# Pacing the row gathers of a two-layer graph attention kernel: a wait for the gather two ahead in place of a memset between gathers

## The chip, the core and the metric

The kernel runs on one core of one Trainium2 chip. The metric is the device time in microseconds (us) of one launch. Engines are named as in the profile: PE is TensorE (PEld its weight loads), DVE is VectorE, ACT is ScalarE, POOL is GpSimd, SP is SyncE. Each engine has an instruction queue of its own; "POOLq" in a row means an instruction that the queue itself handled, such as a wait on a semaphore.

## The reference, cut to what matters

Two graph attention layers run on N = 6250 nodes with D = 256 features and E = 200000 edges, which come sorted by their destination node. Layer 0 has four heads, layer 1 has one. For each edge the layer needs the transformed row of the source node:

```python
hx = (x @ Wg).reshape(n, h, f)
al = leaky_relu(s_src[src] + s_dst[dst] + s_edge, 0.2)      # one logit per edge and head
m = segment_max(al, dst)
al = exp(al - m[dst])
al = al / segment_sum(al, dst)[dst]
out = segment_sum(hx[src] * al[:, :, None], dst)             # the rows of all sources, weighted
x = out + b + x                                              # layer 0 has a relu around it
```

The edge term comes from a small network on 32 edge features. Each node also has a loop edge to itself, whose edge feature is the mean over its incoming edges.

## The kernel before, in words

A prologue writes, for every node, one table row into device memory: `T0` for layer 0 (268 floats: the 256 features of `hx` and a few scalars), later `T1` for layer 1 (260 floats are read of each row). The edges are then worked through in steps of `P * C` = 128 x 24 edges. There are 66 steps in each layer; the last two are shorter (14 and 13 chunks). An edge of a step lies on one of 128 partitions, in one of 24 chunks.

`gather(st)` fetches the table rows of a step's source nodes into a tile `G` of 128 x 24 x 270 floats. It issues one indirect DMA per chunk from the POOL queue (L799): 128 rows, one for each partition, named by a column of the index tile `src`. The last chunk of a step goes first, then chunks 0 to 22. After each such gather, POOL runs a memset of a scratch tile `gap`, 128 x 208 floats (L803), that nothing reads. The very first step is not gathered from the table: the prologue fetches its rows of `x` with 24 indirect DMAs of its own (L249), without memsets between them. So L799 runs 3102 times in all.

There are three buffers for `G` (`gp[k % 3]`). The whole schedule is written out by hand; each engine takes its instructions in program order. In the loop of `edges`, the gather of step k+1 is issued first. Then come the logits of step k on DVE (L987 is the first instruction that reads `G`), the scans and the running maxima per destination, the scaling of the gathered rows in place (L1095, DVE, it writes columns 0 to 255 of `G`), and the sums as 24 matmuls with one-hot matrices (L1105, PE). ACT copies the sums out of PSUM (L1110), and the finishing work of the step before follows on DVE and ACT. The loads of the coming steps (`ea`, `lb`, `tw`) and the stores of finished rows (`T<-t1row` in layer 0 at L1239, `out` in layer 1) go through SP's queue.

Semaphores are placed by the framework. The gathers go round eight completion semaphores in turn, and a gather's completion counts 16 increments on its semaphore. A gather waits for the gather eight before it, which used the same semaphore; the first one of a step also waits for the last readers of its buffer. Where an instruction has several waits, the last one stands in the instruction itself, and the others are put before it on its queue as `EVENT_SEMAPHORE` instructions; these are seen in the trace as POOLq rows.

Between the layers (`ending`) POOL does the finishing of two steps (14 elementwise instructions, L1178 to L1192), and the first gather of layer 1 waits until `T1` is written. At the end two indirect DMAs on POOL store the last two steps' rows (L1249).

Of the kernel before, what the change touches and what calls it, by code (L numbers as in the profile page):

```python
# [22 lines left out]
F32 = mybir.dt.float32  # L23
# [8 lines left out]
P = 128  # L32
C = 24
SE = P * C
NX = 24
D = 256
ED = 32
PH = 64
# [18 lines left out]
class Layer:  # L57
# [3 lines left out]
    def __init__(self, l):  # L61
        self.l = l
        self.H = H = HEADS[l]
        self.F = D // H
        self.p = D
        self.g = D + H
        self.one = D + H + 1
        self.gr = self.ad = D + H + 2
        self.m = self.ln = D + 2 * H + 2
        self.W = D + 3 * H + 2  # L70
# [9 lines left out]
class Kernel:  # L80
# [122 lines left out]
    def prologue(self):  # L203
# [4 lines left out]
        GT = 7  # L208
        CX = self.CX = min(self.cs[0], NX)
        V = nc.vector  # L210
# [192 lines left out]
    def fixed_rows(self):  # L403
        nc, cp = self.nc, self.cp
        self.crow = cp.tile([1, D + self.L[0].H], F32, name="crow")
        self.cl = [cp.tile([36, P + 1], F32, name=f"cl{i}") for i in range(2)]
        for t in self.cl:
            nc.gpsimd.memset(t, -BIG)

        self.cnt = cp.tile([P, self.NS, 2], F32, name="cnt")  # L410
        self.mt = cp.tile([P, 4 * C + 4], F32, name="mt")
        self.gap = cp.tile([P, 208], F32, name="gap")
        self.fb = [cp.tile([P, 37 * C], F32, name=f"fb{i}") for i in range(2)]
        for t in [self.mt] + self.fb:
            nc.gpsimd.memset(t, 0.0)


        self.aq = [cp.tile([P, 4, 32], BF, name=f"aq{i}") for i in range(2)]
        for t in self.aq:
            nc.gpsimd.memset(t, 0.0)  # L420
        self.trow1 = []
        L1 = self.L[1]
        for i in range(2):
            self.trow1.append(cp.tile([P, 2 * L1.TW], F32, name=f"t1row{i}"))
            nc.gpsimd.memset(self.trow1[i][:, L1.TW + D:], 0.0)
# [366 lines left out]
    def gather(self, st):  # L792
        nc, L = self.nc, st["L"]
        st["G"] = G = self.G0 if st["k"] == 0 else self.gp[st["k"] % 3].tile([P, C, 270], F32, name="G")
        n = self.N
        idx = self.src[:, st["o"]:st["o"] + st["C"]]
        last = st["C"] - 1
        for c in (range(0) if st["k"] == 0 and self.CX > last else (last, *range(last))):
            nc.gpsimd.indirect_dma_start(  # L799
                out=G[:, c, 0:L.TW], out_offset=None, in_=self.rows[L.l][0:n * (1 + L.l), :],  # L800
                in_offset=bass.IndirectOffsetOnAxis(ap=idx[:, c:c + 1], axis=0))
            if st["k"]:
                nc.gpsimd.memset(self.gap, 0.0)  # L803

    def pair(self, k):

# [660 lines left out]
```

## Time and profile before

| | before |
|---|---|
| median of 3 runs | 4556.34 us (4555.35 to 4557.77) |
| the profiled execution: time | 4555.93 us |
| its span | 4554.1 us |
| mean granted TensorE clock | 0.743 |
| POOL busy | 3915.8 us (86%) |
| PE busy | 3065.9 us (67%) |
| DVE busy | 2901.8 us (64%) |
| ACT busy | 516.8 us (11%) |
| gathers of L799 | 3102, from 89.3 to 4511.8 us |
| memsets of L803 | 3102 |
| busy share of the DMA engines by the gathers' queue | 35.2% |
| the same by the queue of SP | 10.0% |

The profile is of one execution. Its time is 1.8 us above its span, and 0.4 us below the median of the runs. Busy time counts an engine's own work; a POOL row for an indirect DMA covers the making of its descriptors, not the moving of the data, which the DMA engines do afterwards. The trace holds the landing of each DMA on its semaphore beside this.

### The profile page before, as it was taken

To read this page: it belongs to the slowest core of one execution; us is meant where nothing else is said; L and a number is where in the kernel's file an instruction comes from. 1 tells how busy PE (TensorE), PEld (TensorE's weight loads), DVE (VectorE), ACT (ScalarE), POOL (GpSimd) and SP (SyncE) were. 2 spreads that over 40 slices of the span, in tenths; PEclk is the share of its full clock that TensorE was granted. 3 is DMA by queue.
4 is the path that set the end of the run, shared out by engine and by line. 5 is a ranking of instruction groups with operands and counts; after the bars stand their busy time and mean duration, and the time that the engine had idled before them with its cause. 6 is when DMAs were issued, how large, how long until landed. Compare 5 with 4: busy or idle time off the path is not lost. (4 is left out here: it accounts for less than half of the span.)

```text
span 4554.1 us, 37613 instructions
## 1 busy us (share of the span) xinstructions
PE 3065.9 (67%) x9916; PEld 1899.5 (42%) x9916; DVE 2901.8 (64%) x6675; ACT 516.8 (11%) x1150; POOL 3915.8 (86%) x6365
## 2 busy tenths in 40 slices
PE   8777677667677677677746566666666665666665
PEld 6444444444444344444424334333343343433433
DVE  7877667677677677676745555555554555555655
ACT  5111111111111111111100000000000000000000
POOL 6888888888888888888878888888888888888885
PEclk9877777777777777777767777777777777777777
DMA  6444444444444444444434444444444444444442
GB/s 224 130 136 134 126 129 136 124 127 136 125 128 135 125 128 135 125 130 134 119 98 124 116 128 122 118 128 128 111 128 121 124 123 128 122 116 122 128 116 74
DMA packets 231112, 576.39 MB, mean 127 GB/s; under 512 B 63097, under 2 KB 87871, under 8 KB 230825
## 3 DMA queue, kind: packets, MB, share of 16 engines
q0 software_dynamic: 150144, 422.75, 35.2%
q1 hardware_dynamic: 80331, 150.52, 10.0%
q8 instruction: 79, 1.29, 0.1%
q14 instruction: 142, 1.16, 0.1%
q10 hardware_dynamic: 416, 0.67, 0.1%
HBM read 542.72 MB, written 31.09 MB: 126 GB/s over the span
## 5 line engine op out<-in xcount | busy, mean ns | idle before, releaser
L799 POOL DMA_INDIRECT G<-T,src x3102 | 2969.6, 957 | 553.1 <-issue 518.7
L1105 PE MATMUL u<-G,S 128*128 128x270 f32 (+1 forms) x6252 | 1461.0, 393 | 106.7 <-DVE G L1085 97.6
L1105 PEld LDWEIGHTS u<-G,S 128*128 128x128 f32 x6252 | 1189.5, 192 | 388.0 <-DVE G L1085 162.1
L803 POOL MEMSET gap<- 128x208 f32 x3102 | 893.3, 288 | 1.8
L1095 DVE TENSOR_TENSOR G<-G,kps 128x6144 f32<-128x6144 f32 (+3 forms) x136 | 853.0, 6274 | 0.0
L885 PE MATMUL y<-ea,webd 64*128 64x384 f32 (+1 forms) x1056 | 749.7, 860 | 67.3 <-ACT R L890 66.7
L1010 PE MATMUL lf<-ident,fb 128*36 128x128 f32 (+1 forms) x132 | 53.3, 404 | 1093.3 <-DVE fb L1002 772.3
L987 DVE TENSOR_TENSOR G<-rt,G 128x96 f32<-128x96 f32 (+1 forms) x132 | 30.2, 228 | 1138.9 <-DMA G<-T,src 1138.6
L1010 PEld LDWEIGHTS lf<-ident,fb 128*36 128x36 f32 (+1 forms) x132 | 15.7, 119 | 1134.6 <-DVE fb L1002 819.2
L899 PE MATMUL zad<-R,wea 128*64 128x384 f32 (+1 forms) x1056 | 476.0, 815 | 0.5 <-DVE aq L952 0.3
L890 ACT ACTIVATE R<-y,webd 128x768 f32<-128x768 f32 x260 | 233.2, 897 | 2015.2 <-PE lf L1027 1647.7
L930 DVE TENSOR_TENSOR S<-kps,loc 128x3072 f32<-128x3072 f32 x132 | 437.5, 3315 | 4.5
L885 PEld LDWEIGHTS y<-ea,webd 64*128 64x128 f32 x1056 | 300.9, 314 | 311.8 <-issue 192.5
L899 PEld LDWEIGHTS zad<-R,wea 128*64 128x64 f32 x1056 | 160.7, 207 | 319.0 <-issue 214.0
L945 PE MATMUL zad<-a,Q 128*128 128x12 bf16 (+1 forms) x132 | 24.9, 188 | 174.6 <-DVE a L943 174.6
L430 PE MATMUL fin<-wg,h1T 128*128 128x260 f32 x264 | 135.3, 667 | 2.3 <-ACT h1T L1200 2.3
L973 DVE STREAM_TRANSPOSE rt<-zad 128x768 f32<-128x768 f32 (+1 forms) x130 | 124.9, 960 | 12.1 <-PE zad L959 11.2
L914 DVE TENSOR_TENSOR lb<-lb,kps 128x1536 bf16<-128x1536 bf16 (+1 forms) x68 | 112.7, 1658 | 0.0
L1110 ACT ACTIVATE U<-u 128x270 f32<-128x270 f32 (+1 forms) x132 | 51.9, 393 | 493.7 <-PE u L1105 493.7
L1041 DVE SCALAR_TENSOR_TENSOR m<-fpen,lf,m 128x24 f32<-128x24 bf16 (+1 forms) x66 | 16.4, 249 | 132.8 <-PE lf L1027 132.6
L945 PEld LDWEIGHTS <-Q 128*128 128x128 bf16 x132 | 13.7, 104 | 208.3 <-DVE a L943 198.6
L430 PEld LDWEIGHTS fin<-wg,h1T 128*128 128x128 f32 x264 | 75.6, 316 | 52.1 <-issue 36.6
(201 smaller groups left out, 2287.5 us busy)
## 6 DMA issues: line engine op xcount, KB each, us to landing
G<-T,src POOLq DMA_INDIRECT x3102, 2.8
ea<-in_ea_dram SPq DMA_DIRECT2D x64, 768.0 KB
lb<-locrow SPq DMA_DIRECT2D x64, 384.0 KB
T<-t1row SPq DMA_DIRECT2D x66, 227.5 KB
tw<-T SPq DMA_DIRECT2D x66, 225.8 KB
tw<-T SPq DMA_DIRECT2D x66, 117.2 KB
tw<-in_x_dram SPq DMA_DIRECT2D x66, 112.0 KB
out_dram<-fb SPq DMA_DIRECT2D x64, 112.0 KB
```

What stands on the lines that cost most here:

```text
L430: self.nc.tensor.matmul(ps[:, :L.MW], hT[:, k, :], self.wg[L.l][:, k, :], start=(k == 0), stop=(k == 1))
L799: nc.gpsimd.indirect_dma_start(out=G[:, c, 0:L.TW], out_offset=None, in_=self.rows[L.l][0:n * (1 + L.l), :], in_offset=bass.IndirectOffset ...
L803: nc.gpsimd.memset(self.gap, 0.0)
L885: nc.tensor.matmul(y[:, o], self.webd[l][r, :], ea[r, w], start=True, stop=True)
L890: nc.scalar.activation(R[:, i, :32 * c].rearrange("p (b n) -> p b n", b=2), y.rearrange("p (b n) -> p b n", b=2)[:, :, :16 * c], AF.Relu, ...
L899: nc.tensor.matmul(st["zad"][i * PH:(i + 1) * PH, o], self.wea[l][0], R[:, i, w], start=True, stop=False)
L914: V.tensor_tensor(lb[:, :, :n], lb[:, :, :n], self.k_part.unsqueeze(2).to_broadcast([P, i, n]), op=OP.is_equal)
L930: nc.vector.tensor_tensor(st["S"][:, c0:c1, :], self.k_iota.unsqueeze(1).to_broadcast(w), self.loc[:, o + c0:o + c1].unsqueeze(2).to_broad ...
L973: V.transpose(rv[:, :32 * c].rearrange("p (b n) -> p b n", b=2), z.rearrange("p (b n) -> p b n", b=2)[:, :, :16 * c])
L1010: self.nc.tensor.transpose(self.lf[0:e.shape[1], 1:P + 1], e, self.ident)
L1095: nc.vector.tensor_tensor(v, v, pw[:, c0:c1, :].unsqueeze(3) .to_broadcast([P, c1 - c0, H, L.F]), op=OP.mult)
L1105: nc.tensor.matmul(st["u"][:, :L.W], S[:, i, :], G[:, i, 0:L.W], start=(j == 0), stop=(j == c - 1))
```

## The change

Each gather of L799 from the third on is preceded by a copy on POOL of one element per partition (128 x 1) of the gather issued two before it. The copy reads what that gather wrote, so it must wait until that gather has landed, and POOL takes its instructions in order. The memset after each gather is gone, and `gap` shrinks to 128 x 1. The list `flight` holds the first column of the chunk of each gather that has been issued and not yet been copied from; it runs on over the steps and over both layers.

```diff
+AHEAD = 2
...
-        self.gap = cp.tile([P, 208], F32, name="gap")
+        self.gap = cp.tile([P, 1], F32, name="gap")
+        self.flight = []
...
         for c in (range(0) if st["k"] == 0 and self.CX > last else (last, *range(last))):
+            if len(self.flight) == AHEAD:
+                nc.gpsimd.tensor_copy(self.gap, self.flight.pop(0))
             nc.gpsimd.indirect_dma_start(
                 out=G[:, c, 0:L.TW], out_offset=None, in_=self.rows[L.l][0:n * (1 + L.l), :],
                 in_offset=bass.IndirectOffsetOnAxis(ap=idx[:, c:c + 1], axis=0))
-            if st["k"]:
-                nc.gpsimd.memset(self.gap, 0.0)
+            self.flight.append(G[:, c, 0:1])
```

In the built program the number of gathers stays at 3102. The 3102 memsets are gone and 3100 copies are there. Each copy but the first has two waits, in this order: the completion semaphore of the gather that it reads, and POOL's own semaphore for the copy before it, which wrote the same scratch element. The gathers' own waits for the gather eight before fall away after the first few, since a copy has already waited for it. The scaling on DVE (L1095) gets a wait for POOL, because it overwrites the element that a copy reads. PE, ACT and SP keep their instructions and their order.

## The prediction

> **What bounds the kernel now.** I read the groups of the page first, then POOL's timeline in the middle of the run, then who waits for whom.
>
> ```profile
> PE 3065.9 (67%) x9916; PEld 1899.5 (42%) x9916; DVE 2901.8 (64%) x6675; ACT 516.8 (11%) x1150; POOL 3915.8 (86%) x6365
> ...
> L799 POOL DMA_INDIRECT G<-T,src x3102 | 2969.6, 957 | 553.1 <-issue 518.7
> ...
> L803 POOL MEMSET gap<- 128x208 f32 x3102 | 893.3, 288 | 1.8
> ```
>
> ```profile
> 1005.76 0.29 POOL L803 MEMSET gap<- 128x208 f32 x1
> 1006.21 0.95 POOL L799 DMA_INDIRECT G<-T,src  x1 [0.17 <-issue]
> 1007.15 0.30 POOL L803 MEMSET gap<- 128x208 f32 x1
> 1007.61 0.95 POOL L799 DMA_INDIRECT G<-T,src  x1 [0.16 <-issue]
> ```
>
> POOL repeats one pattern: 0.95 us for a gather, 0.285 for the memset, 0.165 of "issue". The median from one gather's start to the next is 1.403 us. The gathers start from 89.3 to 4511.8 us, 97% of the span, and 3101 x 1.403 = 4351 of those 4422 us are this pattern. The 24 chunks of a step take 33.7 us; DVE and PE need 22 and 24 us for a step (2901.8 and 3065.9 over 130 steps). So POOL sets the pace, and the waits show it from the other side:
>
> ```profile
> DVE G L987 <- DMA G<-T,src: 1138.6, 128, 24.3
> ...
> POOL G L799 <- issue: 518.7, 3096, 2.0
> ```
>
> DVE waits about 8.9 us in each step for the last gather; POOL waits for practically nobody. Whatever is added to or taken from the time between two gathers therefore counts some 3100 times in full, until a step falls under 24 us (1.0 us per gather).
>
> **What the change takes away.** The memset. It does not free 0.45 us: the prologue's gathers have no memset between them, and still start 1.25 us apart.
>
> ```profile
> 11.16 0.95 POOL L249 DMA_INDIRECT G<-in_x_dram,src  x1 [0.30 <-issue]
> 12.41 0.95 POOL L249 DMA_INDIRECT G<-in_x_dram,src  x1 [0.30 <-issue]
> ```
>
> So at most 0.15 us per gather is to be had, and the copy takes a part of that back: the nearest row is the copy of 128x2 to 128x7 elements in the prologue, 0.19 us at every size. Without any real wait the period would be 0.95 + 0.19 + 0.16 = 1.30 us.
>
> **What the change adds: a wait for the landing.** Gather i may not start before gather i-2 has landed, its copy has run, and its own start-up is over. If L is the time from a gather's start to its landing and w the time from that landing to the start of gather i, two gathers take L + w, and the period is the larger of 1.30 and (L + w)/2.
>
> L is in the trace, by line:
>
> ```profile
> L799 POOLq EVENT_SEMAPHORE  x138: 17/43/6385, 71.1 to 4493.4; - x138
> ...
> DMA to landing us min/median/max: 2.7/2.8/8.2
> ```
>
> Over all 3102 landings the minimum is 2.68, the median 2.80, the mean 3.30 us. The floor is narrow, so I do not expect it to shrink with fewer gathers in flight. Already (2.80 + 0)/2 = 1.40 is today's period: any w at all is a loss. A rule to weigh here is in the Trainium skill, page "DMA: Bandwidth & Descriptors", section "Anatomy of one DMA — SWDGE (gpsimd) path": a fixed 2.0 us, mostly the receipt at the end, plus the bytes at 436 GB/s. For 128 rows of 1072 bytes that estimates 2.31 us, against 2.68 at the least here; it makes the same point that a pipelined stream hides a latency which a wait exposes.
>
> w is the term that decides. A copy has two waits (the landing, then POOL's own semaphore). Where an instruction has more than one, the others stand before it as EVENT_SEMAPHORE rows of POOL's queue, the 138 above; the landing will be such a row, and it stops the queue. Gathers that began after such a stop show what it costs: the queue had not prepared the gather behind it. One was released by a matmul that ended at 157.81 + 4.04 = 161.85, one by a landing that released SP's next load at 2309.00:
>
> ```profile
> 157.81 4.04 PE L1105 MATMUL u<-G,S 128*128 128x270 f32 x17
> ...
> 162.62 0.95 POOL L799 DMA_INDIRECT G<-T,src  x1 [5.81 <-ACT U L1110]
> ```
>
> ```profile
> 2309.00 2.01 SPq L866 DMA_DIRECT2D tw<-T  x3
> 2309.75 1.06 POOL L799 DMA_INDIRECT G<-T,src  x1 [10.18 <-DMA T<-t1row]
> ```
>
> (ACT is named in the first since it ended last; G's readers there are PE's.) Both give 0.75 to 0.77 us; the first table gather and the last store, by the ends of their event rows, 0.86 and 0.79. In the steady stream this preparation runs under the gather before, which is why only 0.165 us of it is seen. The new copy stands between stop and gather. Its 0.19 us can run beside the preparation; it costs nothing if so, 0.19 if the preparation starts only when it ends. I take 0.06 (an estimate nearer the first end, as the queue hands instructions over ahead). So w = 0.77 + 0.06 = 0.83, from 0.77 to 0.96.
>
> Base: (2.80 + 0.83)/2 = 1.815 us, 0.412 more than 1.403, x 3100 = **+1277 us**.
>
> **Late landings.** 26% of the gathers land more than 0.25 us above 2.85, in some 190 clusters, while SP's loads and stores use the DMA engines. Today that is covered: a gather waits only for the one eight before. With two in flight it stops POOL. Half the sum of all lateness over 2.85 (each late landing delays one of two interleaved chains) is 766 us. But a cluster lasts as long as SP's transfers, and the slower stream puts fewer gathers into it; counting only the latest gather of each cluster gives 455 us. I take **+455**, and keep 766 for the range; little below 455 fits, since a landing late by e stops POOL by about e.
>
> **The rest.** Gathers that took longer to generate (24 us in all) lie under the new wait: -24. Behind the waiting copy on POOL stand only gathers, the 14 elementwise instructions between the layers and the two last stores. Those come after the last copy of their layer, whose landing is 1 to 2 us old by then: nothing. DVE's scaling now waits for the copies of chunks 21 and 22, which run within 4 us of the landing that starts L987, and the first scaling started 7.8 us after the first L987: nothing; uncovered it would be 4 us in each of 130 steps, but DVE has the 8.9 us of slack to absorb that. The head (89 us), the tail (42 us) and the 42 us hole between the layers stay.
>
> Sum: 4555.9 + 1277 + 455 - 24 = 6264 us against the profiled execution. That execution lies 0.4 us below the median of the runs, so the forecast stays **6264 us**.
>
> **Rivals.**
>
> *The preparation stays hidden.* If the wait for the landing sits in the copy itself, or the queue prepares the gather while the stop lasts, w is a wake-up of 0.07 (a POOL operation of the prologue started 0.07 us after its semaphore), the copy's 0.19 and the 0.16 of issue: 0.42. Then the period is 1.61, and 0.207 x 3100 = 642, + 455 - 24: **5629 us**. For it: the first of the two last stores had its only pending wait in the instruction and began 0.28 us after the DVE memset that released it. Against it: the four starts of 0.75 to 0.86, and the order of the copy's waits. By the Trainium skill, "Perfetto Trace Analysis", section "DMA Instruction — SWDGE (GPSIMD)", an instruction waits in a queue of its own and the sequencer goes on to decode the next, which would give this case; those four starts speak against it for waits that come as event rows. 0.20.
>
> *All terms at their upper ends.* w = 0.96 and every late landing in full: 0.477 x 3100 = 1479, + 766 - 24: **6777 us**. For it: lateness by gather number is what the trace has; against it, the slower stream. 0.12.
>
> *The landing comes sooner with only two in flight.* The sixteen increments of a gather arrive spread out, the first at a median of 2.46 us; if less traffic let all of them come then, the base is (2.46 + 0.83)/2 = 1.645: 0.242 x 3100 = 750, + 455 - 24: **5737 us**, within my range. Against it: the prologue's last four gathers, with little else moving, landed in 2.7 to 2.9 us. 0.03. By the 2.31 us that the Trainium skill's section on one DMA leads to, the sum would be 5505 us; no landing here is that short.
>
> *The copies hardly wait: faster.* POOL would run at 1.30 us, 0.103 x 3100 = -319: **4237 us**; DVE and PE, at 24 us per step, would not stop it. It decides where L + w falls under 2.81: with w = 0.42 that is L = 2.39, about where the first of a gather's 16 increments lands (median 2.46) and not the last. For it: 55% of the gathers already start after gather i-2 has landed. Against it: no landing came under 2.68, and the wait counts all 16. That the change does not do what it says would look the same. 0.04. A cancellation to within 0.2% of the time (what a measurement of this kernel can tell from no change) needs a period right to 0.003 us: 0.01.
>
> **The numbers.** Forecast 0.60, its own range 6170 (w = 0.77) to 6680 (w = 0.90 and 766 us of late landings). Rivals 0.20, 0.12, 0.03 and 0.04; no change 0.01. The range reaches down to 5540 to take in the hidden preparation with a floor of 2.75, and up to 6680; it leaves out half of the case with all terms high, the faster one, no change and the tails of the first two, 0.2 in all. Slower: 0.95.
>
> **What would show it.** In the changed profile: the gaps before L803's gathers grow to about 0.86 us (1.815 less 0.95), with the copies' event rows in them; landings stay at a median of 2.8; from landing to the next gather but one 0.83; DVE's wait at L987 grows by some 13 us per step. A gap near 0.65, and 0.42 from landing to start, would be the first rival. The forecast is wrong if the median period is under 1.7, or if landings fall clearly under 2.68.

## The result and the profile after

The changed kernel takes 6266.35 us (median of 5 runs, 6264.37 to 6268.54); the kernel before takes 4555.35 us beside it (5 runs). The ratio is 1.3756, with a 95% interval of 1.3741 to 1.377. The forecast was 6264 us. The profiled execution has a span of 6264.5 us, and its lines that answer to those shown of before are these. First, from the page, the engines' busy times and POOL's two groups (busy time, mean ns of one, then the idle time just before them and what ended it):

```profile
PE 3070.2 (49%) x9916; PEld 1897.8 (30%) x9916; DVE 2883.5 (46%) x6675; ACT 516.6 (8%) x1150; POOL 3679.6 (59%) x6363
...
L803 POOL DMA_INDIRECT G<-T,src x3102 | 3023.9, 975 | 1273.6 <-issue 1190.7
...
L802 POOL COPY gap<-G 128x1 f32<-128x1 f32 x3100 | 596.0, 192 | 1231.9 <-DMA G<-T,src 1211.4
```

PE and DVE do the same work as before. POOL's busy time fell by 236 us: a copy of 0.19 us stands where a memset of 0.29 stood (297 us less in all), while the gathers took 54 us more. But its idle time before these instructions rose from 555 us to 2506 us, in two nearly equal halves: before the copies, nearly all of it ended by a landing, and before the gathers, marked "issue". The timeline of POOL shows both halves together at every second gather; at the one between, the landing has come while POOL still made the gather before, and the copy follows at once:

```profile
1005.38 0.18 POOL L802 COPY gap<-G 128x1 f32<-128x1 f32 x1 [0.37 <-DMA G<-T,src]
1006.07 0.97 POOL L803 DMA_INDIRECT G<-T,src  x1 [0.50 <-issue]
1007.05 0.19 POOL L802 COPY gap<-G 128x1 f32<-128x1 f32 x1
1007.64 0.97 POOL L803 DMA_INDIRECT G<-T,src  x1 [0.40 <-issue]
1009.00 0.18 POOL L802 COPY gap<-G 128x1 f32<-128x1 f32 x1 [0.38 <-DMA G<-T,src]
1009.68 0.97 POOL L803 DMA_INDIRECT G<-T,src  x1 [0.50 <-issue]
```

After these copies, 0.50 or 0.40 us pass before the gather, where 0.165 us passed after a memset. From two answers on single lines: the copies' waits did come as rows of POOL's queue, and the landing is what it was.

```profile
L802 POOLq EVENT_SEMAPHORE  x3098: 17/17/17, 91.8 to 6221.7; - x194
```

```profile
DMA to landing us min/median/max: 2.7/2.8/8.0
```

The wait of DVE for the gathers, from the list of waits, grew by (2873.0 - 1138.6)/130 = 13.3 us for each step:

```profile
DVE G L990 <- DMA G<-T,src: 2873.0, 131, 37.0
```

The terms of the sum can be measured from the trace's starts and landings. The time from the landing of gather i-2 to the start of gather i is 0.808 us from the 5th to the 75th percentile. The median landing is 2.81 us after the start. Half the time from one gather to the next but one has the median 1.815 us.

The trace also shows what the 0.808 us consist of. Nearly every event row of the copies (some 3000 of 3098) starts 0.024 us after the landing and lasts 0.017 us; the waiting itself is not in the row's time. In the usual case the next gather starts 0.767 us after the end of the row. It does so whether the copy between them began 0.125 us after the landing (the roughly 1600 copies that POOL stood waiting for) or, with POOL still busy, 0.33 to 0.50 us after it (the middle half of the others). So the start of the gather hangs on the release of the row, and not on the copy.

### The profile page after: what moved, and what is told of

Its sections match the earlier page's. It is cut to its first block, busy times and chain, and to the rows that moved or that the text cites. A ratio compares the mean times of both kernels' runs of the same rounds, so it can differ in the third digit from the quotient of the medians.

```text
span 6264.5 us, 40704 instructions
## 1 busy us (share of the span) xinstructions
PE 3070.2 (49%) x9916; PEld 1897.8 (30%) x9916; DVE 2883.5 (46%) x6675; ACT 516.6 (8%) x1150; POOL 3679.6 (59%) x6363
## 3 DMA queue, kind: packets, MB, share of 16 engines
q1 hardware_dynamic: 80331, 150.52, 7.4%
## 5 line engine op out<-in xcount | busy, mean ns | idle before, releaser
L803 POOL DMA_INDIRECT G<-T,src x3102 | 3023.9, 975 | 1273.6 <-issue 1190.7
L990 DVE TENSOR_TENSOR G<-rt,G 128x96 f32<-128x96 f32 (+1 forms) x132 | 30.3, 229 | 2873.0 <-DMA G<-T,src 2873.0
L802 POOL COPY gap<-G 128x1 f32<-128x1 f32 x3100 | 596.0, 192 | 1231.9 <-DMA G<-T,src 1211.4
L432 PE MATMUL ps<-wg,hT 128*128 128x266 f32 x292 | 80.1, 397 | 5.5 <-ACT hT L318 5.5
L962 PE MATMUL zad<-lb,aq 128*128 128x384 bf16 (+1 forms) x264 | 81.7, 400 | 0.0
```

What stands on the lines that cost most here:

```text
L432: self.nc.tensor.matmul(ps[:, :L.MW], hT[:, k, :], self.wg[L.l][:, k, :], start=(k == 0), stop=(k == 1))
L802: nc.gpsimd.tensor_copy(self.gap, self.flight.pop(0))
L803: nc.gpsimd.indirect_dma_start(out=G[:, c, 0:L.TW], out_offset=None, in_=self.rows[L.l][0:n * (1 + L.l), :], in_offset=bass.IndirectOffset ...
L962: self.nc.tensor.matmul(st["zad"][:, o], st["aq"].rearrange("p k j -> p (k j)"), st["lb"][:, w], start=False, stop=True)
```

## The experiments

Each kernel ran against the kernel before on the same chip. The kernel before had medians of 4554.9 to 4555.8 us beside them, so the rows can be set against one another. The last columns are from the profiled execution of each: the usual period (the median of half the time from a gather to the next but one) and what the mean period lies above it, times 3101. 36 to 46 us of the latter are the hole between the layers, in every row.

| kernel | time, us | ratio to before (95% interval) | usual period, us | above it, us |
|---|---|---|---|---|
| before (memset) | 4555 | 1 | 1.403 | 71 |
| changed, two ahead | 6266 | 1.3756 (1.3741 to 1.377) | 1.815 | 507 |
| e1: copy without a wait | 4350.5 | 0.9549 (0.953 to 0.9568) | 1.326 | 106 |
| e2: wait inside the copy | 5711.3 | 1.2536 (1.2511 to 1.2561) | 1.616 | 569 |
| e3: three ahead | 4802.7 | 1.0545 (1.0528 to 1.0563) | 1.323 | 562 |
| e4: nothing between | 4092.9 | 0.8984 (0.8969 to 0.8999) | 1.251 | 82 |
| f1: fewer loads | 6020.7 | 1.3219 (1.318 to 1.3257) | 1.818 | 250 |
| f3: memset kept | 6326.6 | 1.389 (1.385 to 1.393) | 1.825 | 535 |
| g1: one ahead | 11789.9 | 2.5885 (2.581 to 2.596) | 3.628 | 409 |
| g4: four ahead | 4563.0 | 1.0014 (1.0003 to 1.0026) | 1.326 | 318 |

**e1, the copy without its wait.** The copy reads a constant tile.

```diff
-            if len(self.flight) == AHEAD:
-                nc.gpsimd.tensor_copy(self.gap, self.flight.pop(0))
+            if st["k"] > 0:
+                nc.gpsimd.tensor_copy(self.gap, self.ones)
```

> The same copy of 128x1 between gathers, but from a constant tile, so that it waits for no landing. If the wait and not the copy costs the time (theory), POOL runs at 0.97 + 0.19 + 0.16 = 1.32 us per gather, which is also the shortest spacing in the changed kernel: 4556 - 0.083 x 3100 = 4299 us. If the copy as an operation on POOL disturbs the gathers (rival), the period stays near 1.8 us and the time near 6266 us.

It took 4350.5 us with a period of 1.326, as the timeline shows:

```profile
1003.12 0.97 POOL L803 DMA_INDIRECT G<-T,src  x1 [0.15 <-issue]
1004.09 0.20 POOL L802 COPY gap<-ones 128x1 f32<-128x1 f32 x1
1004.44 0.97 POOL L803 DMA_INDIRECT G<-T,src  x1 [0.15 <-issue]
```

The copy as an operation is cheap, cheaper than the memset; the whole loss is the wait. Of the 50 us above the expected time, 35 are in the "above it" column (106 against 71), which the expectation had left out; the rest is the period, 1.326 where 1.32 was expected.

**e2, the form of the wait.** Each copy writes an unused element of its own chunk, so it has no copy before it to wait for.

```diff
-                nc.gpsimd.tensor_copy(self.gap, self.flight.pop(0))
+                nc.gpsimd.tensor_copy(*self.flight.pop(0))
...
-            self.flight.append(G[:, c, 0:1])
+            self.flight.append((G[:, c, 269:270], G[:, c, 0:1]))
```

> As the changed kernel with two ahead, but each copy writes an unused element of its own chunk, so its wait for the copy before it falls away and the wait for the landing is the only one, inside the copy, with no event row before it. Theory (an event row stops POOL's queue, and the preparation of the next gather starts only when it is released): from the landing to the next gather but one 0.42 us in place of 0.81, period (2.81 + 0.42)/2 = 1.61 us, 4556 + 642 + 437 = 5635 us. Rival (the preparation waits for the landing whatever form the wait has): 0.81 us and about 6266 us as before. A second rival (the preparation waits for the copy to be done): 0.26 us more than the first.

The event rows are gone but for two of them (from the answer on L802), and POOL's timeline has a different gap behind the copy:

```profile
L802 POOLq EVENT_SEMAPHORE  x2: 17/17/17, 2891.0 to 2901.2; - x2
```

```profile
1002.20 0.18 POOL L802 COPY G<-G 128x1 f32<-128x1 f32 x1 [0.48 <-DMA G<-T,src]
1002.53 0.97 POOL L803 DMA_INDIRECT G<-T,src  x1 [0.15 <-issue]
```

The copy waits 0.48 us for a landing here, and the gather still follows 0.15 us after it: it had been prepared during the wait. (The profile has no row for this preparation; it is read from the start times.) From the landing to the start of the next gather but one it is 0.395 us (5th to 75th percentile), against 0.808 with the event row. So the first rival of the prediction is real: it is what happens if the wait sits in the copy itself. The edit also takes away the copy's wait for the copy before it, but that one is not what cost the time: the copies of e1 have it too, and their period is 1.326 us. The rule of the Trainium skill ("Perfetto Trace Analysis", section "DMA Instruction — SWDGE (GPSIMD)"), told there of a DMA, is that an instruction waits in a queue of its own while the sequencer goes on to the next. The 0.395 us here, behind a waiting copy, agree with it; with an event row in front, the 0.808 us say otherwise. The time of 5711 us lies 76 us above what was expected, most of it in the last column: 569 - 507 = 62 us more than in the changed kernel.

**e3, g4 and g1: three, four and one ahead.** Only the number is changed:

```diff
-AHEAD = 2
+AHEAD = 3        # 4 in g4, 1 in g1
```

> The changed kernel with three gathers ahead. Theory (period is the larger of 1.32 and (L + w)/n): (2.81 + 0.81)/3 = 1.21 is under 1.32, so POOL is free of the wait except where a landing is over 0.34 us late; 4299 us plus 250 to 400 us for late landings, 4550 to 4700 us. Rival (each landing wait as an event row costs its 0.8 us regardless of how many are in flight): over 6000 us.

> The changed kernel with four ahead. Theory: unhindered as the copy that waits for nothing (4351 us measured, 1.326 us per gather); a landing stops POOL only if it is later than 4 x 1.326 - 0.81 = 4.49 us after the start, so of the 450 us that late landings cost at two and at three ahead 100 to 250 stay, 4450 to 4600 us. Rival (an event row costs something on each gather, however long its semaphore has been there): 4800 us as with three ahead.

> The changed kernel with one gather in flight. Theory (period (L + w)/n with L = 2.81 and w = 0.81): 3.62 us per gather, 4556 + 2.214 x 3101 = 11420 us, with 300 to 600 us of late landings, 11720 to 12020 us. Rival (w is hidden when nothing else is in flight, so 2.81 + 0.42): about 1200 us less.

With one in flight the period is 3.628 us, and 2.81 + 0.81 = 3.62: nothing is hidden, and each copy waits:

```profile
1004.18 0.18 POOL L802 COPY gap<-G 128x1 f32<-128x1 f32 x1 [1.96 <-DMA G<-T,src]
1004.86 0.97 POOL L803 DMA_INDIRECT G<-T,src  x1 [0.50 <-issue]
```

With three and four the usual period is 1.323 and 1.326, that of e1, although the event rows are still there for each copy (3097 of them with three ahead, from the answer on L802). Not all of them find their semaphore there: with three ahead some 2860 still start 0.024 us after the landing, so the landing released them. But there it comes early, usually 1.13 to 1.24 us before the start of the next gather (the middle half), and the 0.81 us that follow it pass under the gather before. With four ahead only some 480 rows start so. An event row costs nothing as long as its landing comes those 0.81 us before POOL is free for the next gather; where it comes later, the preparation is exposed. The list of waits shows how seldom POOL itself stops with three and with four ahead (us in total, times, the longest), where the changed kernel had 1211.4 us in 1609:

```profile
POOL gap L802 <- DMA G<-T,src: 321.1, 250, 3.8
```

```profile
POOL gap L802 <- DMA G<-T,src: 155.4, 131, 3.5
```

The expectation for three ahead was missed: 4803 us against 4550 to 4700. Against e1, the wait costs 452 us there, nearly as much as late landings cost in the changed kernel (507 - 71 = 436), though a gather could be 0.34 us late for free. I had let that slack save too much. Most late landings are over 0.34 us late, and the faster stream puts more gathers into a cluster: 21% of them land late by the prediction's measure with three ahead, 14% with two. With four ahead the cost is still 212 us against e1, and it uses up what the shorter period gives, to within 0.2% of the kernel before.

That these costs are late landings can be reckoned from the traces. Let each gather start at the later of 1.322 us after the last one and 0.808 us after the landing of the one two, three or four before. With the landings as the trace has them, the run then comes out longer than with every landing at 2.85 us or earlier by 412 us for two ahead, 437 for three and 218 for four. These are estimates, and close to the 436, 452 and 212 us above.

**f1, fewer loads.** `ea` and `lb` are loaded for the first steps only, and their tiles are used again. The kernel so leaves out the later steps' own edge features and locations, and does not compute the two layers; the gathers and the instructions of the compute engines keep their numbers.

```diff
+            if not hasattr(self, "ea0"):
+                self.ea0 = self.lp.tile([P, 2, 32 * C], F32, name="ea", bufs=1)
...
+            if k >= 4:
+                for i, st in enumerate(self.pair(k)):
+                    st["lb"], st["lb2"] = self.lbs[k // 2 % 2][:, i], self.lbs[k // 2 % 2]
+                return
```

> The changed kernel with two ahead, but SP's two largest loads, the edge features ea (768 KB for two steps) and the locations lb (384 KB for two steps), are made only for the first steps and their tiles are used again; the edge terms are left out of the result in that way. The step of 437 us that late landings cost is tested. Theory (they are late because SP's loads hold the DMA engines): in the changed kernel's trace 369 of some 395 us of stretched pair times lie within 9 us after an ea or an lb load, alone or with smaller transfers beside it; with those two gone 150 to 330 us go, 5940 to 6110 us. Rival (the gathers' own rows in device memory come late now and then): near 6266 us.

The page's line of SP's queue shows half the bytes (150.52 MB before):

```profile
q1 hardware_dynamic: 53907, 75.27, 4.1%
```

The usual period stayed at 1.818 us, and the time above it fell from 507 to 250 us; the run is 246 us shorter. So over half of what late landings cost (257 us of some 436) follows from SP's two large loads. That the rest follows from the other transfers was not tried.

**f3, the memset kept beside the wait.**

```diff
-        self.gap = cp.tile([P, 1], F32, name="gap")
+        self.gap = cp.tile([P, 208], F32, name="gap")
+        self.one_gap = cp.tile([P, 1], F32, name="one_gap")
...
-                nc.gpsimd.tensor_copy(self.gap, self.flight.pop(0))
+                nc.gpsimd.tensor_copy(self.one_gap, self.flight.pop(0))
...
+            if st["k"]:
+                nc.gpsimd.memset(self.gap, 0.0)
```

> The wait is added and the memset of 128x208 after each gather stays. Theory (with two in flight the memset runs while POOL waits for the landing): no change against the changed kernel, 6240 to 6300 us, although taking the memset out of the kernel before gave 463 us. Rival (the memset's 0.15 us per gather is on the path here too): 6266 + 0.15 x 3100 = 6730 us.

It took 6326.6 us, 60 us above the changed kernel and 27 above the upper end of what was expected. Nearly all of the memset is covered, but not all: the shortest spacing of two gathers (its 1st percentile) rose from 1.32 to 1.54 us, so there is less room to catch up after a late landing (535 against 507 us), and the usual period is 0.01 us longer (some 31 us).

**e4, nothing between the gathers.** The edit is shown against the kernel before; there is no copy either.

```diff
-            if st["k"]:
-                nc.gpsimd.memset(self.gap, 0.0)
```

> Neither memset nor copy between the gathers. From the prologue's gathers: 1.25 us per gather, 4556 - 0.153 x 3100 = 4082 us; a step is then 30 us, above the 24 us that PE and DVE need. Rival (gathers that follow each other without a gap hinder each other in the DMA engines or POOL's own descriptor making, so that the memset pays for itself): 4556 us or more.

It took 4092.9 us, 463 us less than the kernel before, with the period of the prologue's gathers:

```profile
999.87 0.95 POOL L801 DMA_INDIRECT G<-T,src  x1 [0.30 <-issue]
1001.12 0.95 POOL L801 DMA_INDIRECT G<-T,src  x1 [0.30 <-issue]
```

More gathers land late at this pace (32%, against 26% before), but POOL waits for hardly any landing (2.4 us in all). This is the fastest kernel of the table; e1 is the only other one that beats the kernel before. POOL still paces it: DVE waits 709.8 us in it for the gathers, 5.5 us in each step.

## Why the prediction was right, point by point

**The bound.** POOL's time between gathers counts in full, up and down: 1.251 to 3.628 us of period gave 4093 to 11790 us, and PE and DVE never took over.

**The memset.** Its removal was put at 0.15 us per gather at most; e4 measured 1.403 - 1.251 = 0.152. In the changed kernel it saves almost none of that, as it would lie under the wait (f3).

**The wait.** The law that the period is the larger of POOL's own pace and (L + w)/n holds for one to four in flight. L was taken as 2.80, and is 2.81; w was taken as 0.83, and is 0.808. The period came out as 1.815 on both sides, a little by luck: (2.81 + 0.81)/2 is 1.81. The 0.06 us put down as the copy's share of w is not the copy's: the copy runs beside the preparation, whose 0.767 us do not depend on when it begins, and the other 0.04 us lie between the landing and the end of the event row.

**The preparation of the gather behind a stop.** This was the step on which 0.60 and 0.20 of the chance parted. It was taken from four starts in the trace of before, three of them of the 3102 gathers (for two of the starts the trace has 0.83 and 0.76 us from the end of the event row, where the prediction says 0.86 and 0.79). The rows of the changed kernel show it some 2500 times, and e2 confirms it by taking the event row away: 0.41 us less per pair, and a time 555 us shorter.

**Late landings.** Forecast at 455 - 24 = 431 us; measured as 507 - 71 = 436. That 766 was too much for two ahead, and for the reason given, is shown: in the slower stream 439 gathers land late, where 799 did before. That 455 fits so closely is partly luck. The same two counts made on the changed kernel's own landings give 376 us for the latest gather of each cluster and 357 for half of all lateness, so the count by clusters is not a rule for the cost. e3 and g4 show that the amount is not a fixed one, but depends on the pace and on how many are in flight.

**The rivals.** That the copies hardly wait needed a landing of under 2.39 us; none came under 2.70 in the changed kernel. The shorter landing with less in flight did not come: with one in flight the median is still 2.81. By the estimate of 2.31 us from the Trainium skill's page "DMA: Bandwidth & Descriptors", section "Anatomy of one DMA — SWDGE (gpsimd) path", the period with one ahead would have been 3.12 us; the measurement, 3.63, decides.

## What to carry to other kernels

Ask of a wait for an earlier transfer not only how long the transfer takes, but how many are in flight: where that is longer than the engine's own pace, the period is (latency + restart)/n, and n has to be large enough for the late landings, not for the median: with four in flight they still cost 212 us here, and more were not tried. A wait that comes as a row of its own on the queue can also expose the preparation of what stands behind it; the same wait inside the instruction, with the instruction's other waits removed by choosing its operands, had half the restart here (0.395 us) and lost a third less time against the kernel before (1156 us in place of 1711). And where one engine paces a kernel, look first for what it does between its real work that nobody reads: here, taking that out gave 10%.

## What the runs showed of the hardware that was not expected

The two forms of a wait differ by 0.41 us (0.808 and 0.395) for the same kind of landing and a copy of the same size; before, this was the choice between the forecast and its first rival. An event row on each copy costs nothing that can be measured where the landing comes early enough, as three and four ahead show by the period of e1. The granted clock of TensorE went down as the kernel got slower, from 0.772 (e4) over 0.743 (before) to 0.674 (changed) and 0.593 (one ahead), with PE's busy time nearly the same; no experiment was made on why, and PE does not set the pace of any of these kernels.
